# The seam between an attention layer and a convolution layer: smaller last batches, one instruction order for both layers, and one block in the last node group

## The chip, the cores and the metric

The kernel runs on one core of a Trainium2 chip. A core has engines that run side by side, each with its own queue of instructions: PE (TensorE) multiplies matrices, DVE (VectorE) works elementwise, reduces and scans, ACT (ScalarE) evaluates functions and copies with a scale, POOL (GpSimd) here issues indirect gathers and clears memory, and SP issues plain transfers. Engines wait for each other by semaphores. Matrix products go to PSUM, everything else lives in SBUF or in DRAM.

The metric is the time of one execution on the device in microseconds (us), as a median over runs. The profile comes from one profiled execution.

## The reference

A graph of 6250 nodes with 128 features each and 206250 directed edges, sorted by their destination `dst`. Two layers, each with a residual and a normalisation around it:

```python
x = layernorm(x + gat_layer(x, edges, edge_attr_128))
x = layernorm(x + conv_layer(x, edges, edge_attr_4, edge_attr_8))
```

The first layer is graph attention with 8 heads of 16 features, followed by a feed-forward part:

```python
xl = x @ W_l + b_l;  xr = x @ W_r + b_r;  ee = edge_attr_128 @ W_e
m = leaky_relu(xl[src] + xr[dst] + ee, 0.2)
logits = einsum('eho,ho->eh', m, att)
exl = exp(logits - segment_max(logits, dst)[dst])
alpha = exl / (segment_sum(exl, dst)[dst] + 1e-16)
out = segment_sum(xl[src] * alpha, dst) + b_att
h = layer_norm(x + out, g1, be1)
gat_layer = layer_norm(h + gelu(h @ W1 + b1) @ W2 + b2, g2, be2)     # W1: 128 x 512
```

The second is an equivariant convolution. A node's features split into 32 scalars and 32 vectors of 3. Each edge's 8 radial values go through two layers of 64 with a tanh-approximated gelu; that gives four sets of 32 filter values, which multiply the gathered source features and the edge's 4 values; the products are summed over each destination and go through a last linear map:

```python
feat, own = linear(x);  e0, e1 = feat[src]
h = gelu_tanh(gelu_tanh(edge_attr_8 @ M1) @ M2);  w = h @ (Wp_00, Wp_01, Wp_10, Wp_11)
mid = products(w, e0, e1, edge_attr_4)
y = cos(pi/8) * own + sin(pi/8) * (segment_sum(mid, dst) @ W2)
```

## The kernel before

**Units, batches, groups.** The edges are padded to 269 *units* (`NU`) of 768 edges (`UE`), 6 tiles of 128 (`TU`). The nodes are 49 blocks of 128. Units are put together into *batches* of up to 8 (`U`), for the segment maximum; node blocks into *groups* of up to two (`G`). `fast_plan` (L57 to L79) makes both lists. Before, the groups are block 0 alone, then blocks 1 and 2, and so on to 47 and 48; the batches are 3, 4, 6 and then 32 of 8, the last one units 261 to 268. `end` of a batch is the step in which its last logits are made; `done` of a group is the unit after which its sums are complete.

**Attention** (`attention`, L378 to L624) is a loop over steps k, one unit of logits per step, written out in a fixed order. A step emits: `linear(k)`; `load(k+2)`, six indirect gathers (`gather`, L366) on POOL and SP's transfers; `terms(k+1)`, the matrix products of the logits (L420); `sum_up`; for batches whose turn it is `shifts` (L494, with an Exp) and `weights` (L507: products into `ex`, Exp on ACT); `peaks` (L471, four scans over the batch's rows on DVE); `sums` (L536); `parts(k)` and `logits(k)` (DVE L443, L450); `collect` (DVE L561, which adds a unit's sums into the node accumulator `acc`); `messages` (a one-hot at L372, and DVE L532, which multiplies gathered rows by the weights); `rows` (PE transposes at L467 that turn a batch's logits into rows); and node stages. A unit passes messages, sums, sum_up and collect in four successive steps, and it can pass messages only after its batch has passed rows, peaks, shifts and weights: rows in the step after `end`, peaks in the next, shifts and weights in the third. A planner at L565 to L575 writes down the step of each unit's messages (`when`) and of each batch's weights (`due`). One unit's messages stand in a step, two in the last 28 steps (`ENDING`) and after the last logits.

**Node stages** (`nodes`, L648 to L756). A group passes 19 stages, called S0 to S18 here, one for each `yield`: transposes of the accumulator (S0, L688), division and residual (S1), a normalisation (S2 and S3, Sqrt on ACT at L636, scale at L645), its scale and bias (S4), a transposition (S5), two halves of the 512-wide product with Gelu (S6, S7, L715 and L718), the product back (S8, L723), residual (S9), normalisations (S10 to S14), a transposition (S15), the convolution's first linear map (S16, L746 and L747), the store of `FEAT` on SP (S17, L749) and that of `BASE` (S18, L754). `Queue` (L85 to L105) takes them forward: a call of `step` takes each open group one stage on; at most two groups are open (`lanes`), and a new one opens only when the group two before it has ended. `rest` calls `step` until all groups are through. The loop calls `step` once per step, and twice from step 273 on (L622); `rest` follows the loop. The last group's S0 stands in step 277, the step of the last collect; its S17 is in the 16th call of `rest`.

**Convolution** (`convolution`, L759 to L944). It clears its accumulator on POOL (L779), loads its weights on ACT's queue, gathers `FEAT` rows for seven pairs of units ahead (84 gathers), runs the radial part of the first two pairs (`radial`: PE L821, ACT L822, eight stages), then loops over 135 pairs in three parts each: `products` on DVE, `sums`, `filters` (L828), `scale` (ACT L836), the next `radial`, a `fetch` of 12 gathers. Eight buffers hold gathered rows. `finish` (L947 to L978) takes the node groups through the last linear map (L964) and normalisation, and stores the output. It uses the same list of groups.

**Order.** `run` (L980 to L988) puts the two layers into two stretches of `manual_schedule`. In such a stretch each engine gets its instructions in the order in which the program emits them. Where two stretches meet, the scheduler may lay instructions of the second among the last of the first, as far as data and memory allow. In the trace of before the convolution's first radial stages, its clearing of memory and its weight loads stand among the last node stages.

Of the kernel before, what the change touches and what calls it, by code (L numbers as in the profile page):

```python
# [8 lines left out]
F32 = mybir.dt.float32  # L9
BF16 = mybir.dt.bfloat16  # L10
I32 = mybir.dt.int32
AF = mybir.ActivationFunctionType
# [31 lines left out]
HEAD = (3, 4)  # L44
RAW = 4
# [11 lines left out]
def fast_plan(n, e):  # L57
# [4 lines left out]
    cuts = [0, *range(nb % G or G, nb + 1, G)]  # L62
# [8 lines left out]
    head = HEAD if nu > sum(HEAD) else ()  # L71
    left = nu - sum(head)
    rest = (left % U,) if left % U else ()
    batches, u, end = [], 0, -2
    for m in head + rest + (U,) * (left // U):
        u += m
        end = max(u - 1, end + 2)
        batches.append((u - m, m, end))
# [29 lines left out]
class Fast:  # L108
# [269 lines left out]
    def attention(self, acc, xlp, xls):  # L378
# [4 lines left out]
        with ExitStack() as st:  # L383
# [193 lines left out]
            AHEAD = 2  # L577
            ends = {end: b for b, (_, _, end) in enumerate(self.batches)}
# [5 lines left out]
            for k in range(max(when) + 4):  # L584
# [63 lines left out]
    def nodes(self, st, acc):  # L648
# [15 lines left out]
        nc.scalar.dma_start(wfs, a["wfs"])  # L664

        def group(b, g, lane):
# [16 lines left out]
            xs = n1.tile([P, G, D], F32, name="xs")  # L683
            nc.sync.dma_start(xs[:, :g], a["x"][blocks].rearrange("(b p) f -> p b f", p=P))
# [19 lines left out]
            self.norm(h, g, *mv)  # L704
            yield
# [6 lines left out]
            for j in range(0, FF // P, 2):  # L712
# [4 lines left out]
                for i in range(2):  # L717
                    nc.scalar.activation(gt[:, j + i, :g * P], f_ps[:, i, :g * P], AF.Gelu, bias=b1[:, j + i:j + i + 1])  # L718
                yield
# [970 lines left out]
```

## Time and profile before

| what | us |
| --- | --- |
| median of 5 runs | 5572.23 |
| lowest and highest | 5561.93, 5588.42 |
| the profiled execution | 5575.03 |
| its span | 5572.9 |
| last gather of the attention ends | 2738.2 |
| last logits (unit 268) end | 2795.6 |
| last collect ends | 2851.9 |
| last store of FEAT issues | 2893.05 |
| first gather of the convolution | 2895.72 |
| first product of the convolution | 2902.04 |

Times inside the profile are counted from the start of the span. The mean granted clock of PE is 0.73 of full speed. The prediction shows lines of three views: the page (busy time of each engine as a share of the span, and the clock in 40 equal slices), busy time by stretches, and the timeline. A timeline line gives the start, the length, the engine, the line of the kernel, the operation, output and inputs by the program's names, their shapes and how many such instructions follow each other; a bracket at its end gives how long the engine had been idle and what it waited for. `SPq` is a transfer that SP issues; `issue` means that the profile shows nothing that was waited for.

### The profile page before, as it was taken

To read this page: it belongs to the slowest core of one execution; us is meant where nothing else is said; L and a number is where in the kernel's file an instruction comes from. 1 tells how busy PE (TensorE), PEld (TensorE's weight loads), DVE (VectorE), ACT (ScalarE), POOL (GpSimd) and SP (SyncE) were. 2 spreads that over 40 slices of the span, in tenths; PEclk is the share of its full clock that TensorE was granted. 3 is DMA by queue.
4 is the path that set the end of the run, shared out by engine and by line. 5 is a ranking of instruction groups with operands and counts; after the bars stand their busy time and mean duration, and the time that the engine had idled before them with its cause. 6 is when DMAs were issued, how large, how long until landed. Compare 5 with 4: busy or idle time off the path is not lost.

```text
span 5572.9 us, 64757 instructions
## 1 busy us (share of the span) xinstructions
PE 3474.8 (62%) x18497; PEld 2246.9 (40%) x18497; DVE 2875.7 (52%) x7372; ACT 1498.6 (27%) x4554; POOL 3107.7 (56%) x3234
## 2 busy tenths in 40 slices
PE   3576777776776766774551655566566466666656
PEld 2455555555555555553430322233233232333323
DVE  1455555555565555554530544455455455555546
ACT  1112122222122222221230333333333233333334
POOL 6256666656566665565226555556556555565561
PEclk6667777767777777776765777777777777777778
DMA  4444444434444443443311111111111111111110
GB/s 118 131 110 110 109 112 111 113 102 113 109 111 109 114 108 100 112 111 84 79 32 46 46 45 47 48 48 50 48 45 50 46 47 49 47 49 49 47 50 18
DMA packets 290621, 427.98 MB, mean 77 GB/s; under 512 B 122700, under 2 KB 199454, under 8 KB 290254
## 3 DMA queue, kind: packets, MB, share of 16 engines
q0 software_dynamic: 103296, 218.27, 16.6%
q1 hardware_dynamic: 183258, 197.77, 12.0%
q10 hardware_dynamic: 3700, 7.69, 0.4%
q8 instruction: 151, 2.47, 0.2%
q14 instruction: 216, 1.77, 0.1%
HBM read 403.45 MB, written 19.96 MB: 76 GB/s over the span
## 4 chain that ended last, share of the span: by engine, by line
another core or an unknown queue 23%; PE 16%; ACT 10%; issue 6%; DVE 3%; POOL 2%; DMA 1%; DVEq 0%; ACTq 0%; POOLq 0%
PE h_ps L821 7%; ACT v L836 5%; PE w L828 3%; ACT h L822 2%; PE y_ps L884 2%; POOL f L366 2%; PE z L420 1%; DMA f<-fFEAT,fsrc 1%; PE m L542 1%; ACT L822 1%; ACT L636 0%; ACT v L645 0%; DVE pr L443 0%; DVE xl L532 0%
## 5 line engine op out<-in xcount | busy, mean ns | idle before, releaser
L366 POOL DMA_INDIRECT xl<-fXL,fsrc x1590 | 1547.3, 973 | 1148.6 <-issue 408.0
L366 POOL DMA_INDIRECT f<-fFEAT,fsrc x1614 | 1526.6, 946 | 1087.1 <-issue 1037.8
L821 PE MATMUL h_ps<-h,m 128*128 128x384 f32 x540 | 323.2, 690 | 784.5 <-ACT h L822 708.2
L420 PE MATMUL z<-fw,ea 128*128 128x136 f32 x3228 | 675.9, 359 | 199.2 <-issue 99.4
L822 ACT ACTIVATE h<-h_ps 128x384 f32<-128x384 f32 x540 | 265.0, 491 | 1663.2 <-remote 1046.3
L420 PEld LDWEIGHTS z<-fw,ea 128*128 128x128 f32 x3228 | 575.2, 252 | 269.6 <-issue 172.1
L443 DVE SCALAR_TENSOR_TENSOR pr<-z,fattb 128x384 f32<-128x384 f32 x538 | 273.7, 550 | 640.3 <-ACT pr L436 499.4
L847 DVE TENSOR_TENSOR oh<-fl,own_ps 128x128 f32<-128x128 f32 x405 | 113.1, 279 | 906.1 <-remote 884.4
L828 PE MATMUL w<-wq,h 128*128 128x256 f32 x1620 | 562.8, 479 | 0.6 <-issue 0.6
L836 ACT ACTIVATE v<-f,e 128x128 f32<-128x128 f32 x1614 | 500.6, 390 | 11.6 <-DMA f<-fFEAT,fsrc 10.0
L821 PE MATMUL h_ps<-e,m 128*128 128x384 f32 (+1 forms) x540 | 363.4, 769 | 212.0 <-ACT h L822 171.1
L546 ACT ACTIVATE sb<-m 128x128 f32<-128x128 f32 x269 | 74.6, 277 | 1553.4 <-remote 764.5
L821 PEld LDWEIGHTS h_ps<-h,m 128*128 128x128 f32 x540 | 115.6, 246 | 844.5 <-ACT h L822 759.1
L828 PEld LDWEIGHTS w<-wq,h 128*128 128x128 f32 x1620 | 334.7, 229 | 253.1 <-issue 205.0
L542 PE MATMUL m<-xl,oh 128*32 128x136 f32 x3228 | 247.6, 356 | 211.1 <-ACT sb L547 82.0
L884 PE MATMUL y_ps<-v,oh 128*32 128x256 f32 x3228 | 316.4, 468 | 78.5 <-issue 27.5
L423 PE MATMUL z<-xl,fcst 128*128 128x408 f32 x538 | 324.9, 693 | 1.7 <-issue 1.5
L555 PEld LDWEIGHTS m<-fcst,sb 128*128 128x128 f32 x1076 | 195.1, 239 | 311.6 <-ACT sb L547 181.8
L821 PEld LDWEIGHTS h_ps<-e,m 128*128 128x128 f32 (+1 forms) x540 | 140.9, 291 | 378.6 <-ACT h L822 316.7
L435 DVE TENSOR_TENSOR z<-z,xl 128x408 f32<-128x408 f32 x269 | 157.9, 587 | 251.5 <-remote 153.9
L555 PE MATMUL m<-fcst,sb 128*128 128x32 f32 x1076 | 183.6, 303 | 164.7 <-ACT sb L547 126.0
L532 DVE TENSOR_TENSOR xl<-xl,ex 128x384 f32<-128x384 f32 x538 | 271.1, 543 | 6.6 <-ACT s L522 6.6
(152 smaller groups left out, 5037.6 us busy)
## 6 DMA issues: line engine op xcount, KB each, us to landing
ea<-fast_eat_dram SPq DMA_DIRECT2D x269, 384.0 KB
lb<-fLB SPq DMA_DIRECT2D x269, 144.0 KB
f<-fFEAT,fsrc POOLq DMA_INDIRECT x1614
xl<-fXL,fsrc POOLq DMA_INDIRECT x1590
xr<-fXR SPq DMA_DIRECT2D x807, 8.5 KB
e<-fast_e8t_dram SPq DMA_DIRECT2D x16, 384.0 KB
fXR<-pt SPq DMA_DIRECT2D x16, 306.0 KB
fXL<-tb SPq DMA_DIRECT2D x16, 204.0 KB
```

Of the source, the lines that this page charges most:

```text
L366: self.nc.gpsimd.indirect_dma_start(out=to, out_offset=None, in_=table, in_offset=bass.IndirectOffsetOnAxis(ap=self.src[:, g:g + 1], axis=0))
L420: nc.tensor.matmul(z[:, t * ZW:(t + 1) * ZW], lhs[:, e], rhs, start=(t == 0 and lhs is ea), stop=(half == 1 and t == 2 and lhs is oht))
L423: nc.tensor.matmul(z, self.ident, xl[:, :3, :].rearrange("p t f -> p (t f)"), start=False, stop=True)
L443: nc.vector.scalar_tensor_tensor(prs[u][:, 3 * H * k:3 * H * (k + 1), :O], z[:, :, :O], 0.0, self.attb, op0=OP.max, op1=OP.mult)
L532: nc.vector.tensor_mul(v, v, ws[b][0][:, t:t + 3, i * H:(i + 1) * H, None].to_broadcast([P, 3, H, O]))
L542: nc.tensor.matmul(ag[q * W:(q + 1) * W], oh[:, t, :], xl[:, t, :], start=(t < 4), stop=(t + 4 >= TU))
L555: nc.tensor.matmul(nd[:, i, j], sb[:, j], self.s4, start=True, stop=True)
L821: nc.tensor.matmul(ps, m, x[:, s], start=True, stop=True)
L822: nc.scalar.activation((h1s, hs)[k][p][:, s], ps, AF.Gelu_apprx_tanh, scale=sc)
L828: nc.tensor.matmul(w[:, 2 * t:2 * t + 2, :], hs[p][:, e:e + P], wq, start=True, stop=True)
L836: nc.scalar.activation(v[:, 2 * t + i, :D], fs[p][:, e, :], AF.Copy, scale=e4s[p][:, e, 3:4])
L884: nc.tensor.matmul(ys[p][q * W:(q + 1) * W, :2 * D], oh[:, t, i], v[:, 2 * t + i], start=(c == 0), stop=(c == PARTS - 1))
```

## The change

- The list of groups is cut from the other end: two blocks from block 0 on, and the last group is block 48 alone.
- Three last batches of 5, 3 and 2 units (`TAIL`). The batches are then 3, 4, 4, thirty-one of 8, and 5, 3, 2; the last ones end at units 258, 263, 266 and 268. For these three, rows stand in the step `end` itself, peaks one step and shifts and weights two steps later: one step sooner than for the others. The planner writes this down in `begun`, and a new batch's weights go by it. By the lists, the messages of units 251 to 263 stand in steps 262 to 268, those of 264 and 265 in step 269, 266 in 270, 267 and 268 in 271; the last collect is in step 274.
- Node stages go one per step to the end of the loop. `rest` then makes 29 calls where it made 17: the group of blocks 44 and 45 has passed S8 by then, that of 46 and 47 opens in the second call, block 48 in the eleventh, and its S17 is in the 28th.
- The input rows `xs` of the last group are loaded on ACT's queue at the set-up of the node stages, into a buffer of their own.
- The last group asks for the Gelu table after its S3 and for the Sqrt table after its S7.
- Both layers stand in one stretch of `manual_schedule`, so on each engine all of the convolution comes after all of the attention.

```diff
+TAIL = (5, 3, 2)
...
-    cuts = [0, *range(nb % G or G, nb + 1, G)]
+    cuts = [0, *range((nb - 1) % G or G, nb, G), nb]
...
-    head = HEAD if nu > sum(HEAD) else ()
-    left = nu - sum(head)
+    head, tail = (HEAD, TAIL) if nu > sum(HEAD + TAIL) else ((), ())
+    left = nu - sum(head + tail)
     rest = (left % U,) if left % U else ()
     batches, u, end = [], 0, -2
-    for m in head + rest + (U,) * (left // U):
+    for m in head + rest + (U,) * (left // U) + tail:
...
-            when, due, k = {}, {}, 0
-            for u in range(NU):
-                b, i = of[u]
-                end = self.batches[b][2]
-                if i == 0:
-                    due[max(k, end + 3), k < end + 3] = b
-                    k = max(k + 1, end + (4 if end < NU - 1 else 3))
-                busy = {k - 2, k - 3} & {b[2] for b in self.batches}
-                if len(when.get(k, ())) == (2 if k >= NU or k > NU - ENDING and not busy else 1):
-                    k += 1
-                when.setdefault(k, []).append(u)
+            when, due, begun, k = {}, {}, {}, -1
+            for b, (v, m, end) in enumerate(self.batches):
+                late = b < len(self.batches) - len(TAIL)
+                begun[end + late] = b
+                w = end + late + 2
+                due[max(k, w), k < w] = b
+                k = max(k + 1, w + late)
+                for u in range(v, v + m):
+                    busy = late and {k - 1, k - 2} & set(begun)
+                    if len(when.get(k, ())) == (2 if k > NU - ENDING and not busy else 1):
+                        k += 1
+                    when.setdefault(k, []).append(u)
...
-                if k - 3 in ends:
-                    shifts(ends[k - 3])
+                if k - 2 in begun:
+                    shifts(begun[k - 2])
...
-                if k - 2 in ends:
-                    peaks(ends[k - 2])
+                if k - 1 in begun:
+                    peaks(begun[k - 1])
...
-                if k - 1 in ends:
-                    rows(ends[k - 1])
-                for _ in range(1 + (k > NU + 3) if k > 1 else 0):
+                if k in begun:
+                    rows(begun[k])
+                if k > 1:
                     nodes.step(max(got, default=-1))
...
+        lb, lg = self.groups[-1]
+        xl = nw.tile([P, lg, D], F32, name="xlast")
+        nc.scalar.dma_start(xl, a["x"][lb * P:(lb + lg) * P].rearrange("(b p) f -> p b f", p=P))
...
-            xs = n1.tile([P, G, D], F32, name="xs")
-            nc.sync.dma_start(xs[:, :g], a["x"][blocks].rearrange("(b p) f -> p b f", p=P))
+            last = b == lb
+            if last:
+                xs = xl
+            else:
+                xs = n1.tile([P, G, D], F32, name="xs")
+                nc.sync.dma_start(xs[:, :g], a["x"][blocks].rearrange("(b p) f -> p b f", p=P))
...
             self.norm(h, g, *mv)
+            if last:
+                nc.scalar.preload_act_table(AF.Gelu)
...
                     nc.scalar.activation(gt[:, j + i, :g * P], f_ps[:, i, :g * P], AF.Gelu, bias=b1[:, j + i:j + i + 1])
+                if last and j + 2 == FF // P:
+                    nc.scalar.preload_act_table(AF.Sqrt)
...
-        with tc.tile_pool(name="frun", bufs=1) as self.fast:
+        with tc.tile_pool(name="frun", bufs=1) as self.fast, tc.manual_schedule():
             with tc.tile_pool(name="xla", bufs=1) as xla, tc.tile_pool(name="xlp", bufs=19) as xlp:
                 acc = xla.tile([P, 2, self.NX], F32, name="acc")
-                with tc.manual_schedule():
-                    self.attention(acc, xlp, self.tables(acc, xlp))
-            with tc.manual_schedule():
-                self.convolution()
+                self.attention(acc, xlp, self.tables(acc, xlp))
+            self.convolution()
```

More of the change, by code (lines that the diff above doesn't have):

```diff
@@ L561, in collect @@
                 nc.vector.scalar_tensor_tensor(v, v, ws[b][1][:, i:i + 1], nds.pop(u), op0=OP.mult, op1=OP.add)
-            when, due, k = {}, {}, 0
-            for u in range(NU):
-                b, i = of[u]
-                end = self.batches[b][2]
-                if i == 0:
-                    due[max(k, end + 3), k < end + 3] = b
-                    k = max(k + 1, end + (4 if end < NU - 1 else 3))
-                busy = {k - 2, k - 3} & {b[2] for b in self.batches}
-                if len(when.get(k, ())) == (2 if k >= NU or k > NU - ENDING and not busy else 1):
-                    k += 1
-                when.setdefault(k, []).append(u)
+            when, due, begun, k = {}, {}, {}, -1
[10 more added lines that the diff above has]
+                    when.setdefault(k, []).append(u)
             AHEAD = 2
-            ends = {end: b for b, (_, _, end) in enumerate(self.batches)}
             for u in range(min(AHEAD, NU)):
```

## The prediction, made before the changed kernel was run

> **What bounds the kernel now.** I read the page first (busy shares, the chain that ended last), then busy time by stretches around the change of layer, then the timeline of that stretch.
>
> The page: no engine is full. Indirect gathers on POOL pace the attention, and the chain goes through several engines:
>
> ```profile
> span 5572.9 us, 64757 instructions
> PE 3474.8 (62%) x18497; PEld 2246.9 (40%) x18497; DVE 2875.7 (52%) x7372; ACT 1498.6 (27%) x4554; POOL 3107.7 (56%) x3234
> ...
> PEclk6667777767777777776765777777777777777778
> ...
> another core or an unknown queue 23%; PE 16%; ACT 10%; issue 6%; DVE 3%; POOL 2%; DMA 1%; DVEq 0%; ACTq 0%; POOLq 0%
> ```
>
> The span holds 269 attention units, about 9.7 us each, then 135 convolution pairs, 19 to 20 us each. The change leaves the work of both as it is and touches the seam between them. Busy time by stretches there (stretch, its us, busy us and count of PE, PEld, DVE, ACT, POOL, granted clock, DMA share, GB/s):
>
> ```profile
> 2735.80:2795.60 59.80, 42.72 (x339) 33.80 (x337) 45.49 (x108) 20.11 (x67) 1.96 (x2) 0.91 0.22 57
> 2795.60:2818.60 23.00, 14.53 (x80) 11.44 (x80) 8.71 (x22) 7.70 (x22) 0.00 (x0) 0.59 0.07 19
> 2818.60:2838.90 20.30, 11.83 (x93) 7.71 (x94) 15.85 (x49) 7.35 (x23) 0.00 (x0) 0.50 0.00 0
> 2838.90:2852.00 13.10, 8.71 (x69) 7.18 (x69) 3.69 (x14) 5.80 (x13) 0.00 (x0) 0.89 0.27 69
> 2857.70:2877.30 19.60, 12.57 (x28) 6.17 (x27) 3.12 (x16) 14.85 (x24) 6.51 (x2) 0.65 0.05 13
> 2877.40:2893.10 15.70, 10.90 (x40) 7.16 (x40) 4.22 (x18) 9.56 (x15) 0.00 (x0) 0.85 0.00 1
> ```
>
> Line 1 holds steps 261 to 268, the last eight units' logits: DVE is 76% busy, POOL has no gather left. Lines 2 to 4 are the way from the last logits to the last collect: DVE 28.3 us of 56.4. Lines 5 and 6 are the last node stages, two groups side by side and then one alone. The timeline gives the order:
>
> ```profile
> 2794.57 1.00 DVE L450 TENSOR_REDUCE lg<-pr 128x48 f32<-128x816 f32 x1
> 2798.90 3.78 PE L723 MATMUL n<-w,gt 128*128 128x128 f32 x16
> 2803.55 0.60 PE L467 MATMUL m<-fcst,lg 128*64 128x128 f32 x4
> 2818.60 1.02 DVE L532 TENSOR_TENSOR xl<-xl,ex 128x384 f32<-128x384 f32 x2 [6.60 <-ACT s L522]
> 2851.28 0.60 DVE L561 SCALAR_TENSOR_TENSOR acc<-acc,s,m 128x64 f32 x2 [1.29 <-issue]
> 2853.57 10.64 POOL L779 MEMSET acc<- 128x6304 f32 x2 [115.32 <-PE n L689]
> 2857.25 1.62 PE L821 MATMUL h_ps<-e,m 128*128 128x384 f32 x2 [3.88 <-DMA m<-fast_m_dram]
> 2871.25 1.28 ACT L718 ACT_TABLE_LOAD   x1
> 2872.55 0.84 ACT L718 ACTIVATE gt<-n,b 128x256 f32<-128x256 f32 x2
> 2893.05 0.36 SPq L749 DMA_DIRECT2D fFEAT<-ft  x1
> 2895.72 0.95 POOL L366 DMA_INDIRECT f<-fFEAT,fsrc  x1 [31.52 <-issue]
> 2902.04 0.30 DVE L865 TENSOR_TENSOR own_ps<-w,f 128x128 f32<-128x128 f32 x1 [8.56 <-DMA f<-fFEAT,fsrc]
> 2947.45 0.49 ACT L822 ACTIVATE h<-h_ps 128x384 f32<-128x384 f32 x1 [34.58 <-remote]
> 3075.23 0.95 POOL L366 DMA_INDIRECT f<-fFEAT,fsrc  x1 [29.72 <-issue]
> ```
>
> Last logits at 2795.6, last collect at 2851.9, last FEAT store at 2893.05 (41.2 us on), first gather 2.7 us later. The convolution's radial stages (L821, L822) already run beside the node stages.
>
> **The change, part by part.** The sum is made against the profiled execution's own 5575.0 us (span 5572.9 and 2.1 around it). That is 2.8 above the median of the runs, 5572.2.
>
> **1. Last batches of 5, 3 and 2.** Before, the last batch is 8 units, 261 to 268, and all its messages come after its last logits. After, the batches end at units 258, 263, 266, 268, and rows, peaks, shifts and weights come one step sooner.
>
> Steps 261 to 268: the logits stay (8 x 3.0 us of DVE: rows .59, 1.01, .41, .99). By the order lists 13 units' messages fall here instead of 8 (+5 x 1.38, from L532 1.02 and L372 0.35) and two batch stages instead of one (+5.24: four scans 3.92, L499 1.12, L501 0.2). Collects and node stages add about 2. DVE goes from 45.5 to 60 us. Idle per step was 1.8 us (14.3 over 8); a denser step hides more of it, the best steps showed 0.8. So 66 to 74 us instead of 59.8: +6 to +14. I take the middle, +10.
>
> Last logits to last collect, before 56.4 us: 8.0 to the rows' transposes (L723's 3.8 us of a node group went first), 15.0 from there to the first message, 20.3 of messages, 13.1 of sums, sum_up and collect. After: the transposes follow the logits in the same step (about 2), the 15.0 stay (scan and Exp latencies; the scans' shape is independent of the batch's size), messages of 2 units remain behind the last weights (3), the last stretch stays at 13.1. That is 33: -23. The low bound takes DVE's own 20 us plus 6 of latency, -30; the high one puts all five late units' messages behind, 6.9 instead of 3, and a full-length row wait, -13. The part: **-13** (-24 to +1). With `late` false the PE's transposes wait on that step's reduction L450, and linear of the next step queues behind them on PE: 2 us for each of three batches, inside the +10.
>
> **2. Single node steps, last group one block.** The doubled steps (before, k above 272) go, so nodes fall behind: at the last collect group 44 has done stage S8; 46 starts at the second closing step, 48 only when 44 has ended, at the eleventh. Its FEAT store is in step 28 of the closing run, before in step 16. Those steps cost: 20 with two groups side by side, 8 of one block alone. Alone, a two-block stage took 1.57 us (15.7 for 10). One-block stages S10 to S17 took 11.6 with two blocks; without the load and half of the two-block instructions (L645, L633, L678, L746, L733 to L735: 3.2) 7.1. Two lanes: no less than 1.57, no more than 3.27 (19.6 us for 6 steps, convolution's work and its table loads among them). I take 2.0, the longer of two paired stages (L723 3.2 with its neighbour, L715 and Gelu 2.1, most others 1.3 to 1.9). 20 x 2.0 + 7.1 = 47, against 41.2: **+6** (-3 to +31).
>
> xs of the last block loaded at the start: the SP load it replaces had a whole lane's time to land; its ACT-queue DMA stands at the start of the node set-up, before anyone waits: 0. If that cover goes, one DMA of the 3.9 us kind (the m wait).
>
> Tables: Gelu is asked for after S3 of group 48 and Sqrt after S7. Group 46's Sqrt stands in the next closing step, so the first preload is turned over: one load more, 1.28 us by the row above, and 0 if ACT idles then; the second hides. The load ends at 2872.53 and its ACTIVATE starts at 2872.55. I put it inside the 2.0.
>
> The Trainium skill ("ScalarE: Activation LUTs", Table sets: the hidden batching unit) says to do all calls of one set before changing, which speaks against a Gelu preload ahead of another lane's Sqrt; by its "What ACT_TABLE_LOAD costs" a switch is 1283 ns and a drain of about 1380 more, 2.66 us. The trace shows the 1283 and no drain behind it (0.02 us). By the page the extra switch would make the sum 1.4 us later.
>
> **3. One fixed order.** Convolution's start moves behind the last node stage on every engine. Cover gone: the m1 wait 3.9 us and eight radial stages of about 1.9 (PE 0.9 to 1.65, ACT 0.49), some 19 us, against a first product that stood 9 us after the FEAT store: about 10 us later. All of it now falls under the gathers, where ACT's waits of 34.6 us show how slowly PE's results are released. Against that, POOL's 120 gathers in a row end in 29.7 us of idle that waits for pair 2; and radial stages, five of their table loads (6.4 us), and the own_ps copy no longer stand between the node stages. In POOL's queue the memset now stands after group 48's S0, 22 us behind the last collect, and is through (10.6) before the store at 47. SP's first e8 load stands behind the last BASE store, ACT's three weight loads behind the last ft. Bounds: -6 (loads no longer switched during the seam) to +25 (the whole 19 and a third again). I take **+2**: of the rows, the 29.7 idle is nearest, since it comes at the point at which the delay would show.
>
> **4. End.** The last finish group has one block: L964 2.08 to 1.04 and half of the two-block ACT and DVE work: **-2** (-1 to -3). **Head**: batches 3, 4, 4 for 3, 4, 6 and a two-block first group, under gathers that pace the steps at 9.7 us: 0 (-1 to +2).
>
> Sum: -13 + 6 + 2 - 2 = **-7**, so 5568 on the profiled execution, 5565 on the median.
>
> **Rivals.**
> - *The last block queues (slower side).* Two-lane closing steps cost as in the row, 3.27 us: part 2 becomes +31, the sum +18, 5590. For it: each group's stage stands in order behind the other's on PE, ACT and DVE, and Sqrt and Gelu still alternate. Against: a third of that row's ACT work is the convolution's. It turns the sign at +13, a step of 2.35 us.
> - *The convolution's start costs.* +25 in part 3: the sum +16, 5588. For: ACT's 34.6 us wait. Against: the 29.7 us idle. It turns the sign at +9.
> - *A larger gain.* DVE binds the tail alone (-24), lanes drift freely (-3), the switches go (-6), -2: -35, 5537. For: DVE at 76% in line 1. Against: the latencies of lines 2 and 4.
> - *Nothing.* What the tail gains, the 28 steps give back: 5572, inside the forecast's own range.
>
> **How the numbers follow.** 0.3%, 16.7 us, is about what a measurement of this kernel can tell from no change. Forecast, -20 to +6, that is 5552 to 5578: 0.46 (0.10 faster, 0.36 same). Larger gain, -17 to -40: 0.24, all faster. Queueing 0.16 (0.04 same, 0.12 slower); convolution's start 0.14 (0.02, 0.02 from a part of it with the gain; 0.10 slower). Together faster 0.36, same 0.42, slower 0.22. The range 5540 to 5592 holds the forecast, the gain to -32 and both slower rivals at their price; 0.05 lies below and 0.12 above.
>
> **What would show it.** Last logits to last collect near 33 us, steps 261 to 268 near 70. Last collect to FEAT store near 47, with group 48's S0 some 20 us behind the last collect. First product about 19 us behind the first gather instead of 6. POOL's gap after 120 gathers at 30 us or more; if it is much longer, or pair 2 ends later against the store than before (180 us), part 3 was wrong. A closing step over 2.35 us makes part 2 wrong; a transposes' wait over 4 us, part 1.

## The result and the profile after

The changed kernel takes 5594.85 us (median of 35 runs, 5567.97 to 5625.56) against 5572.53 (60 runs). The ratio is 1.0037, interval 1.0028 to 1.0046: slower by about 21 us, where 7 us of gain were forecast, and outside the range given. The profiled execution took 5603.4 us.

The page after, the same lines as of before but for the clock:

```profile
span 5601.6 us, 64901 instructions
PE 3493.9 (62%) x18549; PEld 2257.6 (40%) x18549; DVE 2884.7 (51%) x7386; ACT 1492.3 (27%) x4561; POOL 3111.3 (56%) x3234
...
another core or an unknown queue 21%; PE 14%; ACT 10%; issue 5%; DVE 3%; POOL 2%; DMA 1%; DVEq 0%; ACTq 0%; SPq 0%; POOLq 0%
```

The engines do the same work; the span is 28.7 us longer. It splits at two gathers that both kernels have. From the last gather of the attention to the first of the convolution: 157.5 us before, 177.9 after, **+20.4**. Ahead of it the profiled execution after is 11.4 us early, behind it 19.6 us late; the runs further down show that those two are not steady. The 11.4 us are no gain: unit 260's logits end at 2735.8 us in both, and only the last gather ends sooner against them (2726.8 instead of 2738.2). So the convolution's first gather comes 9.1 us later than before (2904.79 against 2895.72), and the larger part of the 28.7 us lies behind it. Busy time by stretches of the changed kernel (stretch, us, busy us and count of PE, PEld, DVE, ACT, POOL, granted clock, DMA share, GB/s):

```profile
2735.80:2809.61 73.81, 53.58 (x393) 42.49 (x393) 53.68 (x117) 24.26 (x81) 0.00 (x0) 0.78 0.17 48
2809.61:2851.71 42.10, 29.20 (x180) 22.20 (x181) 19.85 (x57) 16.66 (x46) 0.00 (x0) 0.50 0.00 1
2851.71:2875.74 24.03, 13.59 (x63) 9.98 (x63) 8.12 (x32) 9.93 (x21) 0.00 (x0) 0.73 0.10 28
2875.74:2901.69 25.95, 9.13 (x31) 6.17 (x29) 9.86 (x42) 13.75 (x26) 10.64 (x2) 0.55 0.04 11
2904.79:3082.24 177.45, 54.92 (x157) 24.47 (x158) 28.68 (x79) 21.21 (x60) 114.46 (x121) 0.58 0.19 50
```

Line 1 is steps 261 to 268 (59.8 us before), line 2 the way from the last logits to the last collect (56.3 before). Together 115.9 against 116.1: the small batches moved 14 us from the second stretch into the first and won nothing. DVE's work in both is the same too, 73.5 us against 73.7. Lines 3 and 4 run from the last collect to group 48's S0 and to its FEAT store: 50.0 against 41.2. Line 5 is the first three pairs of the convolution: 177.4 against 180.6.

The timeline of the same places after:

```profile
2808.61 1.00 DVE L451 TENSOR_REDUCE lg<-pr 128x48 f32<-128x816 f32 x1
2817.59 1.02 PE L468 MATMUL m<-fcst,lg 128*16 128x128 f32 x4 [0.74 <-ACT s L523]
2838.59 1.02 DVE L533 TENSOR_TENSOR xl<-xl,ex 128x384 f32<-128x384 f32 x2 [2.19 <-ACT s L523]
2851.11 0.60 DVE L562 SCALAR_TENSOR_TENSOR acc<-acc,s,m 128x64 f32 x2 [5.14 <-PE m L556]
2875.70 0.29 PE L697 MATMUL n<-fcst,acc 128*128 128x8 f32 x2
2882.69 1.28 ACT L715 ACT_TABLE_LOAD   x1
2883.98 1.28 ACT L638 ACT_TABLE_LOAD   x1
2885.28 0.29 ACT L638 ACTIVATE rs<-mv,feps 128x2 f32<-128x2 f32 x1
2901.69 0.33 SPq L762 DMA_DIRECT2D fFEAT<-ft  x1
2904.79 0.95 POOL L367 DMA_INDIRECT f<-fFEAT,fsrc  x1 [17.79 <-DMA fFEAT<-ft]
2926.23 0.30 DVE L878 TENSOR_TENSOR own_ps<-w,f 128x128 f32<-128x128 f32 x1 [17.88 <-issue]
3062.07 0.95 POOL L367 DMA_INDIRECT f<-fFEAT,fsrc  x1 [22.49 <-issue]
```

Last logits to the last batch's transposes 8.0 us; from there to its messages 21.0; then 13.1 to the last collect. Group 48 opens 24 us behind the last collect (2875.70). The asked-for Gelu table (L715) is turned over by group 46's Sqrt (L638) at once. POOL's first pause comes after 108 gathers and lasts 22.5 us, where it came after 120 and lasted 29.7.

### The profile page after: what moved, and what is told of

Read it like the earlier page. It is cut to its first block, busy times and chain, and to the rows that moved or that the text cites. A ratio compares the mean times of both kernels' runs of the same rounds, so it can differ in the third digit from the quotient of the medians.

```text
span 5601.6 us, 64901 instructions
## 1 busy us (share of the span) xinstructions
PE 3493.9 (62%) x18549; PEld 2257.6 (40%) x18549; DVE 2884.7 (51%) x7386; ACT 1492.3 (27%) x4561; POOL 3111.3 (56%) x3234
## 4 chain that ended last, share of the span: by engine, by line
another core or an unknown queue 21%; PE 14%; ACT 10%; issue 5%; DVE 3%; POOL 2%; DMA 1%; DVEq 0%; ACTq 0%; SPq 0%; POOLq 0%
PE h_ps L834 7%; ACT v L849 5%; PE w L841 3%; ACT h L835 2%; PE y_ps L897 2%; POOL f L367 2%; DMA f<-fFEAT,fsrc 1%; PE m L543 1%; PE z L421 1%; ACT L835 1%; ACT L638 0%; DVE xl L533 0%; ACT v L647 0%; DVE r L882 0%
## 5 line engine op out<-in xcount | busy, mean ns | idle before, releaser
L543 PE MATMUL m<-xl,oh 128*32 128x136 f32 x3228 | 253.6, 360 | 212.2 <-ACT sb L548 67.3
```

The costliest lines, as they stand in the source:

```text
L543: nc.tensor.matmul(ag[q * W:(q + 1) * W], oh[:, t, :], xl[:, t, :], start=(t < 4), stop=(t + 4 >= TU))
```

## The experiments

One plain remark on the times: two kinds of chip answered. On one the kernel before takes 5572 to 5579 us, on the other 4231 to 4241 (its POOL gathers have the same pitch there, 1.25 us; the section on the hardware shows the difference). The kernel before was measured beside every group of runs, on the same chip, so ratios are compared across the groups, and times are not. Where I write "seam", it is the time from the last gather of the attention to the first one of the convolution. Intervals from the timeline, in us:

| kernel | steps 261-268 | to last collect | to last group's S0 | to its FEAT store | seam | ratio to before |
| --- | --- | --- | --- | --- | --- | --- |
| before (5572) | 59.8 | 56.3 | 0.8 | 40.4 | 157.5 | 1 |
| after (5595) | 73.8 | 42.1 | 24.0 | 26.0 | 177.9 | 1.0037 [1.0028, 1.0046] |
| after_oh4 (5586) | 64.2 | 39.3 | 23.8 | 25.9 | 165.4 | 1.0018 [1.0000, 1.0036] |
| best_oh4 (5514) | 60.3 | 48.3 | 3.4 | 30.3 | 143.0 | 0.9888 [0.9869, 0.9907] |
| before_again | 63.1 | 56.3 | 0.8 | 38.5 | 106.8 | 1 |
| before_third | 61.8 | 55.6 | 0.5 | 38.5 | 106.1 | 1 |
| after_again (4254) | 80.5 | 41.3 | 25.0 | 24.6 | 124.8 | 1.0034 [1.0021, 1.0047] |
| after_third (4248) | 77.0 | 41.4 | 25.0 | 24.7 | 120.8 | 1.0026 [1.0017, 1.0035] |
| before_parts | 64.4 | 55.5 | 0.8 | 40.6 | 110.0 | 0.9992 [0.9982, 1.0002] |
| before_tail | 82.9 | 43.5 | 6.6 | 41.1 | 124.2 | 1.0036 [1.0024, 1.0048] |
| before_newcuts | 56.9 | 55.7 | 10.9 | 34.4 | 113.8 | 1.0021 [1.0012, 1.0029] |
| before_one | 63.1 | 55.3 | 0.8 | 31.5 | 100.1 | 0.9983 [0.9975, 0.9992] |
| after_two | 73.1 | 41.7 | 25.0 | 36.8 | 135.2 | 1.0052 [1.0039, 1.0065] |
| after_double | 93.6 | 49.5 | 7.1 | 29.6 | 135.1 | 1.0062 [1.0050, 1.0075] |
| after_oldcuts | 81.9 | 42.4 | 9.9 | 34.4 | 120.5 | 1.0020 [1.0010, 1.0031] |
| after_late | 69.8 | 44.2 | 19.3 | 24.5 | 113.2 | 1.0010 [1.0001, 1.0018] |
| after_notail | 58.4 | 47.0 | 13.3 | 26.9 | 104.4 | 0.9974 [0.9963, 0.9985] |
| notail_parts | 60.0 | 41.2 | 14.0 | 25.2 | 94.0 | 0.9972 [0.9960, 0.9983] |
| notail_oldcuts | 59.7 | 49.8 | 3.6 | 30.0 | 96.9 | 0.9972 [0.9962, 0.9982] |
| best | 63.2 | 49.8 | 3.6 | 30.1 | 97.1 | 0.9973 [0.9962, 0.9984] |

after_notail and notail_parts have the same attention, and their seams are 10 us apart: a single profile's seam is good to about that. Verdicts below rest on the ratios; the intervals tell where the time lies.

### First: is it the convolution's long pairs, or the seam?

In the first two profiles some pairs of the convolution take 25 to 33 us instead of 19, 5 of them before and 7 after. Theory 1: the new cuts put the finish groups onto other pairs and cause them. Theory 2: the loss is in the seam.

```diff
# after_oldcuts, from after
-    cuts = [0, *range((nb - 1) % G or G, nb, G), nb]
+    cuts = [0, *range(nb % G or G, nb + 1, G)]
```

> The changed kernel with the node groups cut as before (block 0 alone first, blocks 47 and 48 last). Theory 1 (the cuts move the finish groups onto other pairs of the convolution, and more pairs take 33 us instead of 19): pairs over 23 us fall from 7 to about 5, pairs 10 to 125 lose some 20 us, and the median falls to 5575 to 5583. Theory 2 (the long pairs come by chance, and the whole loss lies in the seam: closing run 9 us longer, no gain in the tail): the median stays at 5590 to 5598; the last group, two blocks again, even makes the closing run some 5 us longer.

```diff
# before_newcuts, from before
-    cuts = [0, *range(nb % G or G, nb + 1, G)]
+    cuts = [0, *range((nb - 1) % G or G, nb, G), nb]
```

> The kernel before with only the new cuts (two blocks first, block 48 alone last). Theory 1: pairs over 23 us rise from 5 to about 7, and the median to 5583 to 5592. Theory 2: the convolution stays as it was, the last group is some 5 us shorter: 5565 to 5573.

```diff
# after_double, from after
-                if k > 1:
+                for _ in range(1 + (k > NU - 12) if k > 1 else 0):
                     nodes.step(max(got, default=-1))
```

> The changed kernel with node stages called twice per step from step 258 on. Theory 2: group 48 opens soon after the last collect instead of 24 us behind it; the closing run falls from 50 us to 28 to 38 and the median by as much, to 5573 to 5583, if the doubled stages do not lengthen the tail by the same. Theory 1: the same gain in the seam, but pairs over 23 us stay at about 7.

```diff
# after_two, from after
-        with tc.tile_pool(name="frun", bufs=1) as self.fast, tc.manual_schedule():
+        with tc.tile_pool(name="frun", bufs=1) as self.fast:
...
-                self.attention(acc, xlp, self.tables(acc, xlp))
-            self.convolution()
+                with tc.manual_schedule():
+                    self.attention(acc, xlp, self.tables(acc, xlp))
+            with tc.manual_schedule():
+                self.convolution()
```

> The changed kernel with the two stretches of order of the kernel before. Theory 2 with the order as its cause: the convolution's radial stages move beside the closing node stages again, the first product follows the first gather by 6 us, and the median falls by 8 to 15 us. Theory 1: the start of the convolution is worth 0 to 4 us either way, 5590 to 5598.

No pair was long on this chip: all take 15 us, and from the first gather of the convolution to the end all four profiles need 2031 to 2035 us. The loss was there all the same. The new cuts alone cost 0.21%, in the seam: the last group opens 10.9 us behind the last collect instead of 0.8, since it waits for the end of the group two before it, and that one is now complete a block later. The saving of the one-block group is smaller (34.4 us from its S0 to the store instead of 38.5). Theory 1 is not needed for the loss on this kind of chip; my expectation of theory 2 for before_newcuts (a gain) was wrong as well. The old cuts in the changed kernel (after_oldcuts) give 1.0020, between what the two theories had said; the interval, 1.0010 to 1.0031, overlaps that of the changed kernel, so a gain from them is likely there and not certain.

Doubling the node stages brought S0 from 25.0 to 7.1, as expected, and made it worse (1.0062): steps 261 to 268 rose to 93.6 us and the way to the last collect to 49.5. Node stages in those steps are not free; what leaves the closing run returns there, and more. With two stretches the changed kernel is slower still (1.0052): convolution's radial stages laid among the closing node stages make these 36.8 us instead of 24.6. So the one stretch looks like a gain, where I had expected it to be worth 0 to 4 us either way, or to be the loss itself; the intervals of 1.0052 and of the changed kernel overlap, and before_one below settles it.

### Second: which part?

> The changed kernel once more, beside the others of this call. Theory A (the loss is the seam: the last block opens late behind two groups, and the small batches win nothing): last collect to the store of FEAT 48 to 54 us, step 240 to the store 10 to 25 us longer than in the kernel before, the median 15 to 28 us above it. Theory 1 (long pairs in the convolution make most of it): on a chip whose pairs take 15 us without long ones, as in the runs so far, the loss is under 10 us.

> The kernel before once more, for its profile beside the others. Theory A: last logits to last collect 52 to 58 us, last collect to the store of FEAT 38 to 44, step 240 to the store some 300 to 312 if the pairs take 15 us.

```diff
# after_notail, from after
-TAIL = (5, 3, 2)
+TAIL = ()
```

> The changed kernel without the three small last batches (the last ones are 8 units again; all else as changed). Theory A, with the batches as neutral: logits of 261 to 268 fall back to 55 to 62 us, last logits to last collect rises to 54 to 60, the closing run stays at 48 to 54; the median within 6 us of the changed kernel's. Rival B (the batches themselves make the loss, by the scans and products they add): the median falls by 10 to 20 us. The forecast's own view (the batches win 13): it rises by 8 to 18.

```diff
# before_one, from before
-        with tc.tile_pool(name="frun", bufs=1) as self.fast:
+        with tc.tile_pool(name="frun", bufs=1) as self.fast, tc.manual_schedule():
...
-                with tc.manual_schedule():
-                    self.attention(acc, xlp, self.tables(acc, xlp))
-            with tc.manual_schedule():
-                self.convolution()
+                self.attention(acc, xlp, self.tables(acc, xlp))
+            self.convolution()
```

> The kernel before with both layers in one stretch of order, nothing else. Theory A: the radial stages leave the closing node stages (41 us falls to 35 to 38) and stand behind the first gathers (first product 21 us behind the first gather instead of 6): the sum 0 to +12 us. Rival C (the order makes most of the loss): +15 to +25 us. The forecast's view: +2 less the loads, -4 to +4.

The changed kernel is slower here too (1.0034), with the same places as on the first chip. Without the small batches it turns to a gain, 0.9974: rival B, the batches, holds (its reason, the added scans and products, is not shown by this run). Two things change in the table: steps 261 to 268 lose 22.1 us and give 5.7 back on the way to the last collect, and the last group opens 13.3 us behind the last collect instead of 25.0. The second was not in my forecast of the batches: the changed kernel's loop has 275 steps and this one's 279 (one more than the kernel before, since the last batch's messages also come a step later), so more of the node stages stand behind it, and block 48 opens in the eleventh closing step instead of the eighth. One stretch alone gives 0.9983, below all three ranges that I had written: the closing run falls from 39.3 to 32.3, and no loss shows at the convolution's start. First gather to pair 10 is 154.6 us against 154.4, though the first product stands 21.3 us behind the gather instead of 6.4. POOL's first 120 gathers set that time on this chip, and the late radial stages fit under them.

### Third: why the small batches cost

```diff
# after_late, from after
-                late = b < len(self.batches) - len(TAIL)
+                late = True
```

> The changed kernel with its batches of 5, 3 and 2, but their rows, peaks, shifts and weights one step later, as for all other batches. Theory D (the small batches themselves cost: two more passes of scans and products on engines that are full in these steps): steps 261 to 268 stay 15 to 22 us longer than with batches of 8, last attention gather to first convolution gather within 6 us of the changed kernel's. Theory E (the stages a step sooner cost, since PE's and DVE's queues stand behind them): steps 261 to 268 lose 8 us or more, and that stretch falls by 8 to 15 us.

before_tail takes the planner and the batches of the changed kernel into the kernel before, with its cuts, its doubled stages and its two stretches:

```diff
# before_tail, from before
+TAIL = (5, 3, 2)
...
+    for m in head + rest + (U,) * (left // U) + tail:
...
+            for b, (v, m, end) in enumerate(self.batches):
+                late = b < len(self.batches) - len(TAIL)
...
+                if k in begun:
+                    rows(begun[k])
```

> The kernel before with the batches of 5, 3 and 2 and their sooner stages alone; cuts, doubled node stages and the two stretches as before. Theory D or E: last attention gather to first convolution gather 10 to 22 us longer than in the kernel before, the median 10 to 22 us higher (0.2 to 0.5%). The forecast's view of this part alone: 13 us lower.

notail_oldcuts joins the edits of after_notail and after_oldcuts.

> The changed kernel without the small batches and with the old cuts: one stretch, single node stages, the two early loads. If the cuts cost by the turn at which the last group opens, group 47 opens 0 to 4 us behind the last collect instead of 13 and the stretch between the gathers is 96 to 102 us: the median 0 to 6 us below the kernel without the small batches. If the one-block last group is worth what it saves (7 us of stages, 2 at the end), it is 2 to 8 us above it.

```diff
# notail_parts, from after_notail; f is then read as fs[p, c] in scale and products
-                f = fs[p] = ld.tile([P, 2 * TU, D], F32, name="f", bufs=FB)
-                for t in range(TU):
-                    for i in range(units(p)):
-                        self.gather(f[:, 2 * t + i, :], self.FEAT, 2 * p + i, t)
+                for c in range(PARTS):
+                    f = fs[p, c] = ld.tile([P, 2 * CT, D], F32, name="f", bufs=FB * PARTS)
+                    for t in range(CT):
+                        for i in range(units(p)):
+                            self.gather(f[:, 2 * t + i, :], self.FEAT, 2 * p + i, c * CT + t)
```

> The changed kernel without the small batches, and with the convolution's gathered rows in buffers of a third of a pair, so that POOL's gathers run in bursts of 4 instead of 12. Where a pair takes 15 us, which is POOL's own 12 gathers of 1.25, nothing changes: within 4 us of the kernel without the small batches. Where a pair takes 19, since PE's completions are seen only when a burst of gathers has ended, the bursts are shorter and a pair falls to 16 to 18: 130 us or more faster.

The small batches alone make the kernel before 0.36% slower, as much as the whole change does. With their stages a step later the changed kernel is at 1.0010 instead of 1.0026 to 1.0037, with steps 261 to 268 at 69.8 us instead of 77.0 to 80.5: the "step sooner" (theory E) costs some 0.2%. The larger part stays. Without the batches the kernel is at 0.9972 to 0.9974, so batches whose stages come as late as all others still cost 15.6 us (4237.29 against notail_parts' 4221.72 on the same chip), and steps 261 to 268 are 11.4 us longer with them than without (58.4).

after_late moves more than the stages. By the lists, 12 units' messages instead of 13 stand in steps 261 to 268, and its loop is a step longer, so the last group opens 19.3 us behind the last collect instead of 25.0. Half of the 7.2 us by which its steps are shorter than after_third's is DVE work that went behind the last logits (50.2 us busy against 53.8, and then 23.7 against 19.8). Why the sooner stages cost the rest is not shown. Without the batches the cuts make no difference that can be told (0.9972 and 0.9974): the last group then opens 3.6 or 13.3 us behind the last collect, and what the old cuts save there the two-block stages cost again. The gathered rows in thirds change nothing where a pair takes 15 us, as expected.

### Fourth: a second pair of profiles, and a faster kernel

> The changed kernel again. If the seam makes the whole loss: 14 to 24 us above the kernel before, with last attention gather to first convolution gather 15 to 22 us longer, whichever length the pairs have. If the long pairs have a share where pairs take 19 us: 20 to 35 us above it, with at least two more pairs over 23 us than in the kernel before.

> The kernel before again, for its profile beside the others: last attention gather to first convolution gather 102 to 112 us where a pair takes 15 us, 150 to 160 where it takes 19, and then 4 to 6 pairs over 23 us.

> The kernel before with the convolution's gathered rows in buffers of a third of a pair. Where a pair takes 15 us: within 5 us of the kernel before. Where it takes 19 with bursts of 12 gathers: shorter bursts, no pair over 23 us, 16 to 18 us a pair, 130 us or more faster.

best is notail_oldcuts with the gathered rows in thirds.

> One stretch of order, single node stages and the two early loads, but the old batches and the old cuts, with the gathered rows in thirds. Where a pair takes 15 us: 8 to 14 us below the kernel before (0.2 to 0.35%), from the seam alone. Where it takes 19: those and what before_parts gains.

after_third repeats the loss (1.0026), with a seam 14.7 us longer than before_third's, both a little under the ranges that I had written. From the first gather of the convolution to the end it needs 2036.1 against 2036.8; between after_again and before_again it was 2031.6 against 2033.0. On this kind of chip the whole loss lies ahead of the convolution's first gather. best is 0.27% faster than before, 10.6 us by the medians, and its seam is 9.0 us shorter than before_third's; the thirds alone (before_parts) give 0.9992, no difference. What the single node stages and the two early loads do alone, no run tells. None of these runs had the first kind of chip, so the long pairs come up again only in the last group.

### Last: what makes the steps of the small batches long

In steps 261 to 268 DVE's idle ahead of the one-hots had grown. The groups of that stretch, of before and then of the changed kernel on the first kind of chip (busy us, mean ns of one, idle us before them and what ended it):

```profile
L443 DVE SCALAR_TENSOR_TENSOR pr<-z,fattb 128x384 f32<-128x384 f32 x16 | 8.1, 550 | 8.5 <-ACT pr L436 8.1 <-issue 0.4
L372 DVE TENSOR_TENSOR oh<-fl,fcst 128x192 f32<-128x192 f32 x8 | 2.8, 355 | 2.4 <-PE m L542 2.4
```

```profile
L444 DVE SCALAR_TENSOR_TENSOR pr<-z,fattb 128x384 f32<-128x384 f32 x16 | 8.1, 548 | 10.3 <-ACT pr L437 9.2 <-ACT sc L503 0.7 <-issue 0.4
L373 DVE TENSOR_TENSOR oh<-fl,fcst 128x192 f32<-128x192 f32 x12 | 4.3, 356 | 9.0 <-PE m L543 9.0
```

A one-hot has two buffers. The third one must wait until PE's sums (L543) have read the first, and all that stands behind it in DVE's queue waits too. Two more buffers take the cause of that wait away:

```diff
# after_oh4, from after (best_oh4: the same in best)
-        oh = pool.tile([P, TU, W], F32, name="oh")
+        oh = pool.tile([P, TU, W], F32, name="oh", bufs=4)
```

> The changed kernel with four buffers for the attention's one-hots instead of two. If DVE's wait for a free one-hot makes the steps of the small batches long: steps 261 to 268 fall by 6 us or more, the median by 5 to 10 us. If PE's queue sets them (5 us more products in steps 261 to 268 to the last collect, at a clock that falls from 0.91 to 0.78): the wait moves to the sums or to the logits' products, the steps stay within 3 us and so does the median.

> The fastest combination so far (one stretch, single node stages, old batches and cuts, gathered rows in thirds) with four one-hot buffers. With batches of 8 the wait was 2.4 us over these steps: 0 to 3 us below that combination, 0.25 to 0.35% below the kernel before.

These two runs had the first kind of chip. The wait is gone; the group and the two stretches of after_oh4:

```profile
L373 DVE TENSOR_TENSOR oh<-fl,fcst 128x192 f32<-128x192 f32 x12 | 4.2, 348 | 0.0
```

```profile
2752.50:2816.71 64.21, 48.80 (x390) 38.20 (x388) 53.12 (x116) 23.98 (x81) 0.00 (x0) 0.85 0.19 55
2816.71:2856.03 39.32, 29.14 (x180) 22.22 (x181) 19.48 (x57) 16.55 (x46) 0.00 (x0) 0.50 0.00 1
```

Steps 261 to 268 take 64.2 us instead of 73.8, and to the last collect it is 103.5 together instead of 115.9. The 9.6 us that the steps lose are the 9.0 us of the wait and 0.6 us of DVE's work (53.7 to 53.1); the wait did not move to another place of DVE's queue (its idle falls from 20.1 to 11.1 us). PE's clock in these steps was 0.85 here and 0.78 in the changed kernel, which could by itself give one-hots back sooner. But after_late had 0.85 in them too, with two buffers, and waited:

```profile
L373 DVE TENSOR_TENSOR oh<-fl,fcst 128x192 f32<-128x192 f32 x10 | 3.5, 353 | 9.4 <-PE m L543 9.4
```

All eight profiles with small batches and two buffers show the wait in these steps, 9.0 to 15.3 us of it; the ten with batches of 8 and two buffers show 1.1 to 6.2. So it comes with the batches, with their stages a step sooner or not.

The ratio is 1.0018 (1.0000 to 1.0036) where the changed kernel's was 1.0037 (1.0028 to 1.0046). The two intervals overlap: the rows show that the wait is gone, the ratios make a gain of some 10 us likely. The kernel still isn't faster than before. Its closing run is 49.7 us as it was, which takes back 8.5 of the 12.6 us that it is ahead at the last collect; the rest is not placed (see What stays open).

best_oh4 is 1.1% faster than the kernel before (0.9888), 5514.1 us against 5578.79, and with that the fastest of all: 14.5 us in the seam (143.0 against 157.5), and 45.8 behind the first gather (2631.4 against 2677.2), where the gathers now run in thirds. No run on this kind of chip has the thirds alone.

## Why the prediction was wrong, step by step

**Part 1, the small batches: the step that failed.** Forecast -13 from unit 260's logits to the last collect; measured -0.2 on the first chip, +2.4 and +1.0 in the two pairs of profiles on the second. Two terms were off, and the first had put the wait for a free one-hot at nothing.

- *Steps 261 to 268*, forecast +10 (6 to 14): +14.0, +17.4, +15.2. I had let a denser step hide more of its idle. DVE's own work there grew by 8 us, not by 14.5: messages, scans and shifts added 11, but the node stages of these steps, which I had let grow, fell from 6.9 to 4.3 us. Its idle grew from 14.3 to 20.1. Behind that is the one-hots' wait: after_oh4 shows that 9.6 of the 14 us go with it, and then the idle does fall, to 11.1. I had counted messages as DVE work with a price, and not as users of a buffer that PE gives back two units later. The "step sooner" has a share too: after_late's steps are 7 to 11 us shorter, and some 4 us of that is work that moved behind the last logits. My reason for a price there, 2 us a batch for PE's queue, is neither shown nor refuted.
- *Last logits to last collect*, forecast 33: measured 42.1, 41.3, 41.4. The transposes came 8.0 us behind the logits and not 2: in PE's queue the sums and the `ex` products of the batch of 3 stand ahead of them. From there to the messages it took 21.0 and not 15.0, with other units' messages and node stages between the scans and the shifts on DVE. From the first of these messages to the last collect it took 13.1, where I had added 3 and 13.1.

With the one-hots' wait taken away the same part gives 103.5 against 116.1, -12.6. That this is almost the -13 of the forecast is luck: its terms are +4.4 and -17.0, and I had +10 and -23. But a gain of that size is there in these two stretches, and the wait for one of two buffers took it.

**Part 2, the closing run**: right in kind, a little small: forecast 47 us and +6; measured 50.0 (+8.8), 49.6 (+10.3), 49.7 (+10.7). The one-block stages at the end took 7.2 (7.1 forecast; 2894.5 to 2901.69). The 20 two-lane steps took 42.8, 2.14 each and not 2.0. The opening of group 48 at the eleventh call of `rest`, 24 to 25 us behind the last collect, came out as read from the lists. What I had not said is that the small batches are a cause of it, by ending the loop three steps sooner than before.

The preload was turned over as forecast, at twice the price that I gave it: the trace has two loads of 1.28 us in a row, and group 46's Sqrt, whose input stood ready at 2882.76 (end of L637), starts at 2885.28. The Trainium skill's rule to group calls by table set ("ScalarE: Activation LUTs", Table sets: the hidden batching unit) spoke against this preload, and the trace agrees; no run leaves the preload out alone. The drain of about 1380 ns that the same page adds to a switch ("What ACT_TABLE_LOAD costs") is not in this trace: the load at 2882.69 starts 0.02 us behind the ACTIVATE ahead of it (2882.18 and 0.49), and the ACTIVATE at 2885.28 starts 0.02 us behind the second load's end.

**Part 3, one stretch**: forecast +2, in truth a gain as a change by itself (0.9983; after_two points the same way from the other side). The start of the convolution lost nothing: the first product stands 21.4 us behind the first gather (19 forecast), and pair 3 comes 177.4 us behind it instead of 180.6. The 29.7 us of POOL's idle, which I had taken as the nearest row, did absorb it, and 22.5 are left of them.

**Part 4**: -2 forecast; -1.5 by the profiles from the last product to the end (-1.1 and -0.6 in the other two pairs). **Head**: 0 forecast, under gathers that pace the steps. On the first chip they do not by themselves: six gathers of 1.25 us make 7.5 of a unit's 9.7 us, and the last one ends 57 us ahead of the last logits (2738.2 and 2795.6).

**Rivals.** The last block's queueing was the nearest to the truth in its place, not in its price: 2.14 us a step, below the 2.35 from which it was to turn the sign by itself. It needed the failed gain of part 1 beside it. The convolution's start did not cost. I gave 0.22 to slower; the range ended at 5592, 3 us short of the median.

**What stays open.** On the second kind of chip the parts make up the loss: in the two pairs of profiles +1.0 to +2.4 from part 1 and +10.3 to +10.7 from part 2, with unit 260's logits 3 to 4 us late. On the first chip they do not. There the parts give about +4 together, and 24 of the profile's 28.7 us lie between the convolution's first three pairs and its last product, where the forecast had no term. In the first two profiles the convolution behind its first gather is 19.6 us longer after; in after_oh4, with the same cuts, it is 2.6 us longer than before. But pairs 10 to 125 alone take 2213.5 us before, 2230.8 after and 2237.0 in after_oh4, so theory 1 stays open on that kind of chip. Pairs 62 and 115 are long in both profiles with the new cuts (33 us) and not in the one with the old cuts on that chip, which speaks for a share of the cuts; pair 9 is long in the profiles of before and after and not in after_oh4, which speaks for chance. On the other chip there are no long pairs, and the loss is there without them. Steps 241 to 260 were longer after, by 10.1, 7.1 and 2.6 us; no run tells why, and two profiles with the old batches differ there by 4.9 (248.0 and 243.1). Scans of three batches fall into them after, and of two before, and the forecast had no term for that.

## What to carry to other kernels

Work that is moved ahead needs free buffers and free places in the queues as much as free engine time: before a stage is advanced, look for the tile that it writes, how many buffers it has, and which engine gives them back. Where stages of a second chain are stepped once per turn of a loop, a shorter loop sends them behind its end; count the calls inside and outside. And when several edits come together, measure each alone: here one was a gain (one stretch), two were losses (the small batches, and the new cuts in the kernel before), and the loss hid the gain.

## What the runs showed of the hardware

On the first kind of chip some of PE's results reach ACT late while POOL issues gathers back to back. A normal pair of the changed kernel (timeline, about 4195 us), and a long one:

```profile
4194.23 0.81 PE L834 MATMUL h_ps<-h,m 128*128 128x384 f32 x2
4199.44 0.95 POOL L367 DMA_INDIRECT f<-fFEAT,fsrc  x1 [0.30 <-issue]
4202.85 0.49 ACT L835 ACTIVATE h<-h_ps 128x384 f32<-128x384 f32 x1 [7.71 <-remote]
...
4234.61 0.81 PE L834 MATMUL h_ps<-h,m 128*128 128x384 f32 x2
4252.00 0.95 POOL L367 DMA_INDIRECT f<-fFEAT,fsrc  x1 [0.30 <-issue]
4257.03 0.49 ACT L835 ACTIVATE h<-h_ps 128x384 f32<-128x384 f32 x1 [24.22 <-remote]
```

In the first, the product ends at 4195.0 by the profile, which models PE's ends; the last of 12 gathers ends at 4200.4, and ACT goes on 2.5 us after that. In the second the next pair's buffers came free within the burst, 24 gathers ran on, and ACT waited 24.2 us. Not every result in a burst is late: in the normal pair the product before that one ends at 4192.29, 6.6 us into the burst, and ACT takes it at 4192.32. So a pair took 12 gathers of 1.25 us and a pause of about 4, 19 us, or 33 where the pause fell out. On the other chip, the same instruction shows no such wait, and a pair takes POOL's 15.0 us. The page's group of it, of before on the first kind of chip, of before_again on the second, and of best_oh4 on the first:

```profile
L822 ACT ACTIVATE h<-h_ps 128x384 f32<-128x384 f32 x540 | 265.0, 491 | 1663.2 <-remote 1046.3
```

```profile
L822 ACT ACTIVATE h<-h_ps 128x384 f32<-128x384 f32 x540 | 261.1, 484 | 417.6 <-PE h_ps L821 416.9
```

```profile
L836 ACT ACTIVATE h<-h_ps 128x384 f32<-128x384 f32 x540 | 263.7, 488 | 1441.0 <-remote 739.1
```

With bursts of 4 gathers between waits the "remote" part falls from 1046 to 739 us, no pair takes more than 23.0, and the convolution is 45.8 us shorter. after_oh4, which has bursts of 12 and the same one stretch of order, keeps 1040.7. My expectation of 130 us or more was too high: three quarters of the pairs still take 19. What holds the completions back, and why one chip shows it and the other not, no run here tells.
